# A recurrent layer on one core: the order in which four interleaved streams issue their operations

## The chip, the core and the metric

The kernel runs on one core of a Trainium2 chip. A core has several engines that run side by side, each through its own queue of instructions, in order: TensorE (PE in the profile; its weight loads are PEld), VectorE (DVE), ScalarE (ACT) and GpSimd (POOL); SyncE (SP) issues most of the transfers. An instruction that needs another engine's result waits at the head of its queue for a semaphore, and all that is behind it in that queue waits too. The metric is the time of one execution on the device in microseconds (us); lower is better.

## The reference

The input x has 256 x 256 positions and 32 channels. Four layers are added to it one after another, each on a group-normalised copy: a gated layer, two Sobel layers, and a recurrent one. The last sets most of the time, and the change is in it. It runs over 256 steps (one for each column of x), on 256 sequences (one for each row), with hidden width 128 and two stacked cells:

```python
z = x_t @ W_lat + b_lat
for j in range(2):
    zz = concatenate([z, h_all[j]], axis=1) @ W_cell[j] + b_cell[j]
    zz = group_norm(zz)                      # 4 groups of 128, one for each gate
    i, f, o, g = split(zz, 4, axis=1)
    c = sigmoid(f) * c_all[j] + sigmoid(i) * tanh(g)
    h = sigmoid(o) * tanh(c)
    z = z + h
x_hat = x_t + z @ W_out + b_out
```

Step t needs h and c of step t-1, so the steps of one cell can't overlap; the two cells and the two halves of the sequences can.

## The kernel before

The recurrence (`recurrence`) works on **four streams**: layer l in (0, 1) times half h in (0, 1) of the sequences, 128 sequences each, on 128 partitions. One step of one stream is a chain of short operations. They have short names, and this document writes the stream behind the name: `sq01` is the square of layer 0, half 1.

- **PE**: `m` multiplies the stream's last hidden state by its recurrent weights (L911), `i` multiplies the hidden state of layer 0 by layer 1's weights (L906, only in streams 10 and 11). Both add into `zz`, one PSUM bank of 128 x 512. `T` transposes by the identity (L963), `to` does so with the output gate (L959, only in the "turned" streams 00 and 10). Once per step `project` (called `x` here, L876 and L879) puts the input's part into the `zz` of all four streams; its matmuls have 32 rows and run four abreast.
- **ACT**: `sq` squares `zz` (L919); `si`, `sf`, `so`, `tg` are the four gates, scaled by the normalisation (L900); `th` is tanh of c (L966).
- **DVE**: `rd` sums the squares of each gate (L924), `ig` = sigmoid(i) tanh(g) (L947), `fc` = sigmoid(f) c (L951), `c` adds the two (L955), `h` = sigmoid(o) tanh(c) (L969 in turned streams, L973 in the others), `e` copies the transposed h out of PSUM (L975, streams 01 and 11). Once per step `hs` adds the h of both layers (L986).
- **POOL**: `pw` raises the sums to the power -1/2 (L927).

In a turned stream c and the output gate are transposed first (`to`, `T`), then tanh and the product are taken; in the others h is computed first and then transposed (`T`, `e`).

Every 8 steps an **output block** is made (`emit`): `o0` multiplies two blocks of the layer's input (L998, one full matmul), `o1` adds the hidden states' part (L1008, matmuls of 32 columns that run four abreast), `of` moves the sum from PSUM to `fin` on ACT (L1017), `ot` transposes it on DVE (L1023), and DMAs on SP's queue store it.

**The order is written by hand.** `PLAN` gives every operation of every stream a moment in us, `PERIOD` the distance of two steps, `OUT` the moments of `x`, `hs` and the output's four parts. All operations of all steps are sorted by these moments and issued in that order; each engine gets its own subsequence. A moment has no other meaning: no operation waits for it. What an operation waits for are semaphores, and what stands ahead of it in its own engine's queue. Moments over PERIOD only mean that the streams are at different steps: at any time stream 11 is two to three steps behind stream 00.

Buffers: the eight PSUM banks are handed out from a list, first in, first out (`bank`, `release`); a `zz` bank comes free with the last of its four gates, a transpose's bank with `h` or `e`, the output's with `of`. Gates, products and tanh have four buffers each (`up`, bufs=4), one for each stream; `sums` and `roots` have 32 slots per stream (`SLOTS`), so from step 32 on `rd` also has to know that `pw` of 32 steps ago has read its slot.

The functions around the change, with the line numbers of the profile:

Of the kernel before, what the change touches and what calls it, by code (L numbers as in the profile page):

```python
# [19 lines left out]
T = 256  # L20
# [723 lines left out]
class RecurrentInputs:  # L744
# [33 lines left out]
    def of(self, t, rows):  # L778
# [5 lines left out]


SLOTS = 32
PERIOD = 7.600
BLOCKS = 2
PLAN = {
    (0, 0): dict(  # L790
        m=0.300, sq=1.814, rd=1.883, pw=2.686, tg=4.187, sf=4.207, so=4.930, fc=5.023,
        to=5.301, si=5.390, ig=5.646, c=5.897, T=6.647, th=7.011, h=7.161,
    ),
    (0, 1): dict(
        m=4.328, sq=5.425, rd=6.234, pw=8.247, sf=8.370, tg=8.501, si=8.549, fc=8.711,
        so=8.739, ig=9.246, c=9.459, th=9.581, h=10.106, T=10.657, e=11.627,
    ),
    (1, 0): dict(
        i=10.749, m=14.225, sq=14.912, rd=15.578, pw=16.964, si=17.174, so=17.198, tg=17.865,
        to=17.992, ig=18.493, sf=18.507, fc=18.957, c=19.359, T=19.440, th=19.713, h=20.542,  # L800
    ),
    (1, 1): dict(
        i=17.550, m=17.552, sq=18.681, rd=19.727, pw=20.540, si=20.935, sf=21.284, fc=21.803,
        tg=21.870, ig=21.907, c=22.633, so=23.115, th=23.210, h=23.269, T=23.489, e=24.537,
    ),
}
OUT = dict(x=7.804, hs=31.517, o0=35.554, o1=38.043, of=39.159, ot=39.669)

def recurrence(tc, out, ident, weights, inputs, general):
# [47 lines left out]
    def at(when, what, *args):  # L859
        todo.append((when, len(todo), what, args))  # L860

    first = {k: min(ops[n] for n in ("i", "m") if n in ops) for k, ops in PLAN.items()}
    ahead = {k: floor((when - OUT["x"]) / PERIOD) for k, when in first.items()}
    streams = sorted(first, key=lambda k: first[k] - ahead[k] * PERIOD)

# [168 lines left out]
    for k in range(inputs.NX, NB // inputs.XT):  # L1034
        at(((k - inputs.NX + 1) * inputs.XT * J + 4.0) * PERIOD, inputs.load, k)
    at(-1e5, busy, 6)
    for n in range(min(ahead.values()), T + max(ahead.values())):
        at(n * PERIOD + OUT["x"], project, n)
    for t in range(T):
        for (l, h), ops in PLAN.items():  # L1040
            for name, when in ops.items():
                at(t * PERIOD + when, one, name, l, h, t)
        at(t * PERIOD + OUT["hs"], both, t)
    for blk in range(0, NB, BLOCKS):
        for part in ("o0", "o1", "of", "ot"):
            at(((blk + BLOCKS) * J - 1) * PERIOD + OUT[part], emit, blk, part)
    todo.sort(key=lambda e: e[:2])
# [45 lines left out]
```

## Time and profile before

| | |
|---|---|
| time, median of 3 runs | 2632.47 us (2629.62 to 2633.8) |
| profiled execution, its own time | 2632.46 us |
| its span, first to last instruction | 2630.6 us |
| granted TensorE clock, mean | 0.991 |
| first `sq00` of the recurrence | 630.6 us after the span's start |
| busy share of the span | PE 98%, DVE 89%, ACT 87%, POOL 49% |
| an ordinary step, from step 32 on (median distance of two `T01`) | 7.51 us |
| an ordinary step before step 32 | 7.37 us |
| a step with an output block, from step 32 on | 9.14 us |
| output blocks | 32, of which the last is made when the streams have ended |

The recurrence thus takes some 2000 us of the 2631. A step has 13 operations of PE (one `x` counted as one), 24 of ACT, 23 of DVE and 4 of POOL, and the same pattern repeats: what holds for one ordinary step and for one output block holds for nearly all. In the timeline that is quoted below, columns are start and duration in us, engine, line, operation, output and inputs, shapes and count, and in brackets the engine's idle time ahead with what ended it.

### The profile page before, as it was taken

Reading aid. Unit: us, or ns where it says so; the run is one execution under the profiler, and the core shown is the slowest. Engines: PE = TensorE matmul, PEld = TensorE weight load, DVE = VectorE, ACT = ScalarE, POOL = GpSimd, SP = SyncE. Lnnn points to the kernel's source line nnn. Section 1 sums busy time; section 2 is a strip of 40 time slices with the busy share of each in tenths; the row PEclk is TensorE's granted clock in tenths of the full one; section 3 lists DMA queues with packets and bytes.
Section 4 is the critical chain, followed back from the end, with each engine's and each line's share of the span. In section 5 each row is a group of like instructions: output and inputs, shape, how many; then the busy total and the mean of one; then the engine's idle time right before and its main releaser. Section 6 shows DMA issues by size and latency. Waiting matters only on the chain.

```text
span 2630.6 us, 43062 instructions
## 1 busy us (share of the span) xinstructions
PE 2574.9 (98%) x11181; PEld 1007.4 (38%) x11181; DVE 2329.4 (89%) x6735; ACT 2296.4 (87%) x6948; POOL 1298.0 (49%) x1288
## 2 busy tenths in 40 slices
PE   7999999998999999999999999999999999999997
PEld 4533433433333333333333333333333333333332
DVE  6788799796999999999999999999999999999996
ACT  5677677675999999999999999999999999999996
POOL 2211276463555555555555555555555555555553
PEclk9899999999999999999999999999999999999998
DMA  4000000002010000001010101010000001000000
GB/s 146 1 1 1 18 1 1 0 1 49 1 25 8 18 12 14 16 10 20 6 21 5 21 5 21 5 24 9 18 12 14 16 10 20 6 5 5 5 5 10
DMA packets 110744, 38.68 MB, mean 15 GB/s; under 512 B 74852, under 2 KB 107653, under 8 KB 110488
## 3 DMA queue, kind: packets, MB, share of 16 engines
q1 hardware_dynamic: 108452, 34.54, 6.1%
q8 instruction: 92, 1.51, 0.3%
q14 instruction: 164, 1.34, 0.2%
q10 hardware_dynamic: 1236, 0.99, 0.1%
q0 software_dynamic: 800, 0.30, 0.1%
HBM read 10.63 MB, written 8.39 MB: 7 GB/s over the span
## 4 chain that ended last, share of the span: by engine, by line
PE 93%; DVE 3%; ACT 2%; POOL 1%; issue 1%; DMA 1%; DVEq 0%; SPq 0%; ACTq 0%; POOLq 0%
PE zz L911 35%; PE zz L906 16%; PE zz L879 8%; PE pt L963 6%; PE pv L315 5%; PE pg L489 4%; PE pg L449 3%; PE zz L876 3%; PE pg L339 2%; PE pt L959 2%; PE pg L315 1%; PE px L1008 1%; PE pc L259 1%; PE px L998 1%; PE pb L280 1%
## 5 line engine op out<-in xcount | busy, mean ns | idle before, releaser
L927 POOL TENSOR_TENSOR rs<-ve,mhalf 128x4 f32<-128x4 f32 x1024 | 1047.1, 1023 | 953.5 <-DVE ve L924 953.5
L911 PE MATMUL zz<-wc,hT 128*128 128x512 f32 x2040 | 1069.0, 612 | 1.4 <-DVE hT L969 1.2
L900 ACT ACTIVATE ga<-zz,rs 128x128 f32<-128x128 f32 x3072 | 974.7, 376 | 53.6 <-POOL rs L927 47.3
L924 DVE TENSOR_REDUCE ve<-sq 128x4 f32<-128x516 f32 x1024 | 705.2, 689 | 69.4 <-ACT sq L919 49.1
L919 ACT ACTIVATE sq<-zz 128x512 f32<-128x512 f32 x1024 | 623.7, 609 | 53.8 <-PE zz L911 14.2
L906 PE MATMUL zz<-wc,hT 128*128 128x512 f32 x1024 | 524.4, 594 | 0.0
L911 PEld LDWEIGHTS zz<-wc,hT 128*128 128x128 f32 x2040 | 306.7, 189 | 355.8 <-DVE hT L969 168.7
L900 ACT ACTIVATE go<-zz,rs 128x128 f32<-128x128 f32 x1024 | 394.1, 385 | 0.0
L947 DVE TENSOR_TENSOR c<-ga 128x128 f32<-128x128 f32 x1024 | 298.4, 291 | 65.1 <-ACT ga L900 58.6
L951 DVE TENSOR_TENSOR fc<-ga,c 128x128 f32<-128x128 f32 x1020 | 297.9, 292 | 5.5 <-ACT ga L900 4.1
L955 DVE TENSOR_TENSOR c<-c,fc 128x128 f32<-128x128 f32 x1020 | 286.7, 281 | 8.8
L879 PE MATMUL zz<-fx,xt 32*128 32x512 f32 x2048 | 265.8, 589 | 0.0
L333 DVE TENSOR_TENSOR o<-pv,sg 128x512 f32<-128x512 f32 x256 | 158.1, 681 | 43.3 <-PE pg L315 37.7
L959 PEld LDWEIGHTS pt<-ident,go 128*128 128x128 f32 x512 | 71.1, 139 | 290.8 <-ACT go L900 283.4
L906 PEld LDWEIGHTS zz<-wc,hT 128*128 128x128 f32 x1024 | 172.7, 209 | 9.4 <-issue 9.4
L963 PEld LDWEIGHTS pt<-ident,c 128*128 128x128 f32 x512 | 70.9, 139 | 268.9 <-DVE c L955 260.9
L966 ACT ACTIVATE th<-c 128x128 f32<-128x128 f32 x512 | 166.0, 324 | 4.6 <-DVE c L955 1.2
L963 PE MATMUL pt<-ident,h 128*128 128x128 f32 x512 | 157.9, 308 | 10.8 <-DVE h L973 8.5
L330 ACT ACTIVATE sg<-pg 128x512 f32<-128x512 f32 x256 | 138.6, 599 | 31.0 <-PE pg L315 26.3
L966 ACT ACTIVATE th<-pt 128x128 f32<-128x128 f32 x512 | 146.2, 286 | 18.9 <-PE pt L963 18.9
L969 DVE TENSOR_TENSOR hT<-pt,th 128x128 f32<-128x128 f32 x512 | 144.1, 282 | 13.8 <-ACT th L966 13.8
L315 PE MATMUL pv<-xb,wv 32*128 32x512 f32 x512 | 156.2, 619 | 0.0
(169 smaller groups left out, 2991.6 us busy)
## 6 DMA issues: line engine op xcount, KB each, us to landing
xt<-xa SPq DMA_DIRECT2D x256, 64.0 KB, 2.0
nat<-in_x_dram SPq DMA_DIRECT2D x16, 512.0 KB, 7.1
out_dram<-st SPq DMA_DIRECT2D x252, 32.0 KB, 1.7
wc<-in_L_conv_W_cell_dram SPq DMA_DIRECT2D x2, 512.0 KB, 4.8
kt<-in_consts_dram ACTq DMA_DIRECT2D x1, 832.0 KB, 6.1
wv<-in_L_conv_Wv_dram POOLq DMA_DIRECT2D x4, 32.0 KB, 4.2
wg<-in_L_conv_Wg_dram POOLq DMA_DIRECT2D x4, 32.0 KB, 6.2
out_dram<-st ACTq DMA_DIRECT2D x4, 32.0 KB, 3.3
```

What stands on the lines that cost most here:

```text
L315: nc.tensor.matmul(ps, lhsT=w[rows, half * P : (half + 1) * P], rhs=mn, start=True, stop=True)
L879: nc.tensor.matmul(v["zz", l, h, t], lhsT=inputs.of(t, r), rhs=fx[r, :], start=False, stop=l == 0 and t == 0,)
L900: nc.scalar.activation(dst, gates(x, g), func, scale=scale)
L906: nc.tensor.matmul(get("zz"), lhsT=v["hT", 0, t][:, seqs], rhs=wc[:, l, 0, :], start=False, stop=t == 0)
L911: nc.tensor.matmul(get("zz"), lhsT=v["hT", l, t - 1][:, seqs], rhs=wc[:, l, 1, :], start=False, stop=True,)
L919: nc.scalar.activation(sqs[l, h][:, :, 0:H], four(get("zz")), AF.Square, scale=float(H**-0.5))
L924: nc.vector.tensor_reduce(ve, sqs[l, h], AX.X, ALU.add)
L927: nc.gpsimd.tensor_tensor(rs, get("ve"), inputs.mhalf, ALU.pow)
L947: nc.vector.tensor_mul(c, gates(get("ga"), 0), gates(get("ga"), 2))
L951: nc.vector.tensor_mul(fc, gates(get("ga"), 1), get("c"))
L963: nc.tensor.transpose(get("pt")[:, 1, 0:P], get("c" if turned else "h"), ident)
L966: nc.scalar.activation(th, get("pt")[:, 1, 0:P] if turned else get("c"), AF.Tanh)
```

## The change

The change gives other moments to the operations. No operation is added, removed or altered.

```diff
-PERIOD = 7.600
+PERIOD = 7.6
 BLOCKS = 2
 PLAN = {
     (0, 0): dict(
-        m=0.300, sq=1.814, rd=1.883, pw=2.686, tg=4.187, sf=4.207, so=4.930, fc=5.023,
-        to=5.301, si=5.390, ig=5.646, c=5.897, T=6.647, th=7.011, h=7.161,
+        m=0.300, sq=0.897, rd=1.315, pw=1.564, sf=2.898, si=3.787, fc=4.372, so=4.652,
+        tg=4.729, ig=5.014, c=5.113, to=5.590, T=6.355, th=6.448, h=6.513,
     ),
     (0, 1): dict(
-        m=4.328, sq=5.425, rd=6.234, pw=8.247, sf=8.370, tg=8.501, si=8.549, fc=8.711,
-        so=8.739, ig=9.246, c=9.459, th=9.581, h=10.106, T=10.657, e=11.627,
+        m=4.745, sq=4.953, rd=5.207, pw=5.217, tg=7.548, sf=7.918, si=8.072, so=8.125,
+        fc=8.561, ig=8.685, c=8.879, th=9.050, h=10.132, T=10.974, e=11.085,
     ),
     (1, 0): dict(
-        i=10.749, m=14.225, sq=14.912, rd=15.578, pw=16.964, si=17.174, so=17.198, tg=17.865,
-        to=17.992, ig=18.493, sf=18.507, fc=18.957, c=19.359, T=19.440, th=19.713, h=20.542,
+        i=11.096, m=13.564, sq=14.380, rd=14.501, pw=14.603, so=16.610, tg=16.973, to=17.142,
+        sf=17.184, si=17.445, fc=18.142, ig=18.269, c=18.830, T=19.003, th=19.210, h=19.658,
     ),
     (1, 1): dict(
-        i=17.550, m=17.552, sq=18.681, rd=19.727, pw=20.540, si=20.935, sf=21.284, fc=21.803,
-        tg=21.870, ig=21.907, c=22.633, so=23.115, th=23.210, h=23.269, T=23.489, e=24.537,
+        i=16.893, m=17.050, sq=17.642, rd=19.345, pw=20.086, si=21.131, sf=21.350, tg=21.355,
+        fc=21.369, ig=21.584, c=21.731, so=22.208, th=22.427, h=23.006, T=23.391, e=23.986,
     ),
 }
-OUT = dict(x=7.804, hs=31.517, o0=35.554, o1=38.043, of=39.159, ot=39.669)
+OUT = dict(x=7.281, hs=31.329, o0=30.902, o1=34.402, of=35.065, ot=35.363)
```

Only the order counts, so the moments are to be sorted. Taken modulo PERIOD they give each engine's order within one step. Each row begins where the lists are easiest to compare and runs round; the output's parts, which come in one step of eight, are in brackets.

```
PE   before  m00      T11 i11 m11 to10 T01 i10 T10      m01 [o0] to00 m10 T00 [o1] x
PE   after   m00 [o0] T11 i11 m11 to10 T01 i10 T10 [o1] m01      to00 m10 T00      x
ACT  before  [of] sq00 si10 th01 so10 tg10 sf10 sq11 tg00 sf00 th10 so00      si00 sq01 si11 sf11 tg11 th00 sq10 so11 th11 sf01 tg01 si01 so01
ACT  after        sq00 so10 th01 tg10 sf10 si10 sq11 sf00 si00 th10 so00 [of] tg00 sq01 si11 sf11 tg11 th00 sq10 so11 th11 tg01 sf01 si01 so01
DVE  before  rd00 h01 ig10 fc10 e01 c10 rd11 fc00 h10      ig00 c00 rd01 fc11 ig11 h00 c11 rd10 h11 fc01 hs ig01 [ot] e11 c01
DVE  after   rd00 h01 fc10 ig10 e01 c10 rd11 fc00 h10 [ot] ig00 c00 rd01 fc11 ig11 h00 c11 rd10 h11 hs fc01 ig01      e11 c01
POOL both    pw00 pw11 pw01 pw10
```

Before, `of` and `ot` of a block are issued in the step after its `o0` and `o1`; after, all four parts are in one step; their moments are 3.6 to 4.7 us earlier.

## The prediction

> **What bounds the kernel now.** I read the page first (busy time, the chain that ended last), then the timeline of one ordinary step, then that of a step with an output block.
>
> ```profile
> PE 2574.9 (98%) x11181; PEld 1007.4 (38%) x11181; DVE 2329.4 (89%) x6735; ACT 2296.4 (87%) x6948; POOL 1298.0 (49%) x1288
> PE 93%; DVE 3%; ACT 2%; POOL 1%; issue 1%; DMA 1%; DVEq 0%; SPq 0%; ACTq 0%; POOLq 0%
> ```
>
> This says PE, but matmuls overlap in the trace, so a busy PE need not be a full one. The timeline of an ordinary step shows what sets its length:
>
> ```profile
> 1238.42 0.30 PE L963 MATMUL pt<-ident,h 128*128 128x128 f32 x1
> ...
> 1239.53 1.02 PE L911 MATMUL zz<-wc,hT 128*128 128x512 f32 x2
> ...
> 1240.65 0.60 ACT L919 ACTIVATE sq<-zz 128x512 f32<-128x512 f32 x1
> ...
> 1241.35 0.69 DVE L924 TENSOR_REDUCE ve<-sq 128x4 f32<-128x516 f32 x1 [0.17 <-ACT sq L919]
> ...
> 1242.58 0.27 DVE L955 TENSOR_TENSOR c<-c,fc 128x128 f32<-128x128 f32 x1
> ...
> 1242.76 1.13 PE L911 MATMUL zz<-wc,hT 128*128 128x512 f32 x2
> ...
> 1242.95 0.31 ACT L966 ACTIVATE th<-c 128x128 f32<-128x128 f32 x1
> 1243.17 0.88 ACT L900 ACTIVATE ga<-zz,rs 128x128 f32<-128x128 f32 x3
> ...
> 1243.73 0.33 PE L963 MATMUL pt<-ident,h 128*128 128x128 f32 x1
> ...
> 1243.93 0.38 ACT L900 ACTIVATE go<-zz,rs 128x128 f32<-128x128 f32 x1
> 1244.18 0.61 ACT L919 ACTIVATE sq<-zz 128x512 f32<-128x512 f32 x1
> ...
> 1244.89 0.69 DVE L924 TENSOR_REDUCE ve<-sq 128x4 f32<-128x516 f32 x1
> ...
> 1245.50 0.28 DVE L973 TENSOR_TENSOR h<-go,th 128x128 f32<-128x128 f32 x1
> ...
> 1245.93 0.30 PE L963 MATMUL pt<-ident,h 128*128 128x128 f32 x1
> ```
>
> Read as a ring: T01 starts at 1238.42; behind it in PE's queue come i10 (+0.14), T10 (+0.86) and m01 (+0.11, 1239.53). m01 ends at 1240.55; sq01 waits for it (1240.65), rd01 for sq01 (1241.35). Behind rd01 stand fc11, ig11, h00 and c11 in DVE's queue (1242.58, ends 1242.85). th11 waits for c11 (1242.95); the gates of 01 and sq00 stand behind it on ACT (1244.18, ends 1244.79). rd00 waits for sq00 (1244.89), h01 stands behind rd00, and T01 waits for h01: 1245.93. **The ring closes after 7.51 us, the step's length**, and has no slack. PE waits in it: the same step's distances without waits (six full matmuls at 0.86, six transposes at 0.11, x with its entry and exit 0.10 + 1.18 + 0.10) sum to 5.16 + 0.66 + 1.38 = 7.20, so PE loses 0.31 per step, most of it ahead of T01.
>
> In a step with an output block another path binds:
>
> ```profile
> 1208.73 1.02 PE L998 MATMUL px<-xa,e 128*128 128x512 f32 x2
> ...
> 1210.56 0.27 PE L963 MATMUL pt<-ident,c 128*128 128x128 f32 x1
> ...
> 1210.76 1.07 PE L1008 MATMUL px<-hs,wout 128*32 128x256 f32 x16
> ...
> 1211.76 0.40 PE L876 MATMUL zz<-fb,sel 32*128 32x512 bf16 x4
> ...
> 1213.04 0.72 ACT L1017 ACTIVATE fin<-px,cst 128x512 f32<-128x512 f32 x1
> ...
> 1213.79 0.71 DVE L1023 STREAM_TRANSPOSE st<-fin 128x512 f32<-128x512 f32 x1 [0.35 <-ACT fin L1017]
> ...
> 1214.17 0.60 ACT L919 ACTIVATE sq<-zz 128x512 f32<-128x512 f32 x1 [0.41 <-PE zz L911]
> ...
> 1215.90 0.30 PE L963 MATMUL pt<-ident,h 128*128 128x128 f32 x1
> ```
>
> o0 takes 0.86 of PE and o1 1.00 (1210.76 to 1211.76), back to back with the rest. T01 comes at 1206.76 and again at 1215.90: 9.14 us, 1.63 over an ordinary step though 1.86 of PE was added; part fell into PE's waits. of and ot cost nothing: of runs while ACT would wait for PE's m00 anyway (sq00 still waits 0.41 after it).
>
> **What the Trainium skill says.** "Perfetto Trace Analysis", Identifying the Most-Contended Engine: matmul busy time is no measure of how full TensorE is. The trace agrees: 98% busy, 0.31 of 7.51 lost. The same page, Identifying Dependency Chains: an instruction that waits for several engines may get extra EventSemaphore instructions ahead of it. Visible here: up to step 31 rd starts 0.03 after its sq (709.56 + 0.60, then 710.19), from step 32 on 0.10, and each rd then has an EVENT_SEMAPHORE ahead of it; the step goes from 7.37 to 7.51 (two rd in the ring, 0.07 each). "TensorEngine Tiling (Array Packing)", Key Properties: a change of tiling mode drains TensorE. Here T00 to o1 takes 0.20 (1210.56 to 1210.76) against 0.11 between untiled instructions, and m00 after x holds PE for 0.97 instead of 0.86. "SBUF — State Buffer", Who interferes with whom: a VectorE instruction with two SBUF inputs and a GpSimd instruction that reads SBUF block one another. At most pw11 shows it, 1.09 at 1239.93 against 1.01 for the other three; 0.08, and not in the ring.
>
> **The change, part by part.**
>
> *Ordinary steps.* Take each link of the ring into the new order. PE: T01, i10, T10, m01 unchanged. DVE: rd01, fc11, ig11, h00, c11 unchanged; rd00, h01 unchanged. ACT: between th11 and sq00 stand the same four gates, tg01 ahead of sf01 instead of behind it. All other links are data. So the ring has the same instructions, and **the ordinary step can't become shorter than 7.51** unless a wait itself becomes cheaper. Could another path become longer?
> - so10 goes from third to first behind sq00, 0.45 earlier. to10 waits less, but T01 behind it still waits for h01: gain 0.
> - so10 is then the first to need pw10, which ends at 1237.06, 0.09 before si10 starts now: covered, and if it weren't, ACT would lose under 0.1 ahead of sq11.
> - si10 goes behind sf10, and fc10 and ig10 swap with it: c10 has the same four gates ahead of it. tg00 goes last of stream 00 and takes si00's place ahead of ig00: same again. Both hidden; without this cover 0.25 each (one gate).
> - hs ahead of fc01: 0.34 sooner on DVE, fc01 later by as much; e11, c01 and rd00 have the same work ahead. If ig01 came late, rd00 (0.07 of idle before it) would slip.
> - An extra event wait may come to th01, since the gate that opens stream 10 is now another one: 0.07, against 0.03 of room behind, and 0.25 until h01 needs it. I take 0.
>
> Sum for ordinary steps: 0, bounds -0.02 and +0.02.
>
> *o0* is moved from behind m01 to behind m00. It now delays T11, i11, m11, to10 and T01. T01 to m00 is 4.34 (1238.42 to 1242.76); then m00 0.97, o0 0.86, T11 0.11, i11 0.86, m11 0.86, to10 0.11: T01 to T01 is 8.11, that is **+0.60**. VectorE is ready by then: T11's turn is 1.83 after m00, e11 is done 0.63 later (as e01 after T01, 1238.42 to 1239.05), then c01 0.20, rd00 0.60, h01 0.20: 3.46, and T01's turn is 3.77.
>
> *o1* is moved from between T00 and x to between T10 and m01, **into the ring**. T01 to m01 becomes i10's 0.11 + 0.86 + 0.20 (T10, with the change of mode) + 1.00 (o1) = 2.17 against 1.11: **+1.06**. Leaving o1's mode may cost m01 another 0.10, as x does to m00; see below.
>
> *of and ot* now follow o1 at once, ahead of tg00 on ACT and of ig00, c00 and **rd01** on DVE. From the turn of m01: o1's recorded end +0.07, of starts 0.12 later (the last block, where ACT was idle: 2621.38 to 2621.50), takes 0.72, ot starts 0.03 later and takes 0.71: 1.65. Behind it ig00 (+0.20), c00 (+0.33, it waits for ig00), rd01 (+0.60): rd01 ends 2.78 after m01's turn. Ordinarily it ends 2.51 after (1239.53 to 1242.04). **+0.27**; the possible 0.10 on m01 lies under it (2.61). Bounds: with ot hidden only that 0.10 stays; with ACT or DVE later than I count, 0.40.
>
> Queues: of's wait for o1 holds up tg00 and sq01 on ACT; tg00 is through 0.91 + 0.26 = 1.17 after m01's turn, and sq01 waits for m01 until 1.12 to 1.22 anyhow. On SP only the output's eight DMAs move with ot; x's loads have steps of room. POOL keeps its order.
>
> *Sum.* After, a block costs 0.60 + 1.06 + 0.27 = 1.93; before, 1.63: **+0.30**. 31 blocks run inside the recurrence: 9.3 us. In the first three the step is 0.14 and sq01 to rd01 0.07 shorter, so they cost 2.14 after against 1.71 before (9.08 less 7.37), 0.13 more each: 0.4. The last block stands alone at the end in both orders. Together +9.7, on the profiled 2632.46 (2630.6 and 1.9 around it), which equals the median 2632.47: **2642 us**, 0.37% slower.
>
> **The rivals.**
> - *Of and ot hidden after all* (13%): the block costs 1.66 to 1.76, +0.03 to +0.13, 1 to 4 us: 2633.5 to 2637, no change. For it: DVE stands still ahead of ot anyway. Against: rd01 is behind ot in the queue.
> - *A double wait leaves the ring* (9%), the faster side: th11 starts 0.10 after c11's end where th01 starts 0.03 after c01's (1214.88 to 1214.91), an event wait's price; if the new order spares it (or one of sq01, rd, T01), 0.07 x 225 steps = 16 us, more than the 9.7: 2626. It decides from 0.06 per step. Against: each of these has the same predecessors in the new order.
> - *A double wait enters the ring* (8%): +16, 2658, the same arithmetic.
> - *The order has no effect* would need o1 outside the ring; its new place is read off the list.
>
> **How the numbers follow.** The forecast has 70% (2638 to 2647). Range 2635 to 2649: the forecast, the nearer half of the hidden case and some of the extra waits. A run can't tell less than about 0.2% (5.3 us) from no change. Faster 0.09, same 0.14, slower 0.77.
>
> **What would show it.** Ordinary T01 to T01 still 7.51 (else the ring argument falls); the block's excess 1.9 over the two steps that it touches; rd01 right behind c00 with ot ahead of ig00; o1 between T10 and m01. An ordinary step off by 0.03 would make the forecast wrong.

## The result, and the profile after

The kernel after takes 2642.98 us (median of 7 runs, 2636.38 to 2648.2), beside 2631.05 us for the kernel before (also 7 runs). The medians are 11.9 us apart; the ratio, taken over all runs, is 1.0036 (95% interval 1.0026 to 1.0046), 9.5 us slower. Its profiled execution took 2636.38 us, with a span of 2634.5 us. Measured again later beside more runs of the kernel before, the ratio was 1.0022 (1.0014 to 1.0030), 5.8 us.

Runs of one kernel differ with the TensorE clock that each was granted. Of the 20 runs of the kernel before in the second measurement, the seven at 0.991 have a median of 2631.3 us, the six at 0.989 one of 2636.3. **At equal clock the kernel after is about 7 us slower**: 7.5 at 0.991 (2638.8, seven runs), 6.9 at 0.989 (2643.2, four runs). In the first measurement four of its seven runs had 0.989, with a median of 2643.0, so at that clock it took the same time in both. The 2631.05 beside it is what the kernel before takes at 0.991; the clocks of those runs, the profiled one (0.991) apart, are not on record. So the 9.5 seems to be in part a difference of granted clocks.

The page of the kernel after says as little as that of before: first the engines' busy times, then the chain that ended last.

```profile
PE 2579.5 (98%) x11181; PEld 1012.0 (38%) x11181; DVE 2318.2 (88%) x6735; ACT 2304.8 (87%) x6948; POOL 1282.6 (49%) x1288
...
PE 93%; DVE 3%; ACT 2%; POOL 1%; issue 1%; DMA 1%; DVEq 0%; SPq 0%; ACTq 0%; POOLq 0%
```

The timeline of one ordinary step of the kernel after (start, duration, engine, line, operation) shows the ring again, link by link:

```profile
1238.01 0.30 PE L963 MATMUL pt<-ident,h 128*128 128x128 f32 x1
...
1239.12 1.02 PE L911 MATMUL zz<-wc,hT 128*128 128x512 f32 x2
...
1240.24 0.60 ACT L919 ACTIVATE sq<-zz 128x512 f32<-128x512 f32 x1
...
1240.94 0.69 DVE L924 TENSOR_REDUCE ve<-sq 128x4 f32<-128x516 f32 x1 [0.18 <-ACT sq L919]
...
1242.17 0.27 DVE L955 TENSOR_TENSOR c<-c,fc 128x128 f32<-128x128 f32 x1
...
1242.54 0.31 ACT L966 ACTIVATE th<-c 128x128 f32<-128x128 f32 x1
1242.75 0.88 ACT L900 ACTIVATE ga<-zz,rs 128x128 f32<-128x128 f32 x3
...
1243.76 0.61 ACT L919 ACTIVATE sq<-zz 128x512 f32<-128x512 f32 x1
...
1244.48 0.69 DVE L924 TENSOR_REDUCE ve<-sq 128x4 f32<-128x516 f32 x1
...
1245.08 0.28 DVE L973 TENSOR_TENSOR h<-go,th 128x128 f32<-128x128 f32 x1
...
1245.51 0.30 PE L963 MATMUL pt<-ident,h 128*128 128x128 f32 x1
```

From `T01` (1238.01) to `T01` (1245.51) is 7.50 us, and 7.51 before. `m01` comes 1.11 behind `T01`, `sq01` 1.12 behind `m01`, `rd01` 0.70 behind `sq01`: the same distances as before, so the new order left the ring alone.

The two steps with an output block, again from the timeline of the kernel after:

```profile
1508.83 0.30 PE L963 MATMUL pt<-ident,h 128*128 128x128 f32 x1
...
1514.12 1.02 PE L998 MATMUL px<-xa,e 128*128 128x512 f32 x2
...
1516.91 0.27 PE L963 MATMUL pt<-ident,h 128*128 128x128 f32 x1
...
1517.88 0.27 PE L963 MATMUL pt<-ident,c 128*128 128x128 f32 x1
...
1518.09 1.07 PE L1008 MATMUL px<-hs,wout 128*32 128x256 f32 x16
...
1519.09 1.13 PE L911 MATMUL zz<-wc,hT 128*128 128x512 f32 x2
1519.22 0.69 ACT L1017 ACTIVATE fin<-px,cst 128x512 f32<-128x512 f32 x1 [0.50 <-PE px L1008]
...
1519.94 0.71 DVE L1023 STREAM_TRANSPOSE st<-fin 128x512 f32<-128x512 f32 x1 [1.09 <-ACT fin L1017]
...
1520.31 0.60 ACT L919 ACTIVATE sq<-zz 128x512 f32<-128x512 f32 x1
1520.58 0.25 DVE L947 TENSOR_TENSOR c<-ga 128x128 f32<-128x128 f32 x1
...
1520.86 0.29 DVE L955 TENSOR_TENSOR c<-c,fc 128x128 f32<-128x128 f32 x1
1521.07 0.68 DVE L924 TENSOR_REDUCE ve<-sq 128x4 f32<-128x516 f32 x1
...
1525.64 0.30 PE L963 MATMUL pt<-ident,h 128*128 128x128 f32 x1
```

The step with `o0` takes 8.08 (1508.83 to 1516.91), the step with `o1`, `of` and `ot` 8.73 (to 1525.64). Together they are 1.80 over two ordinary steps, where a block cost 1.64 before: 0.17 more (1.803 less 1.637), 31 times, is 5.2 us. From the first `T01` of the recurrence to the last it is 1971.2 us after and 1964.2 before, in the profiled executions: 7.0 us.

### The profile page after: what moved, and what is told of

The parts are those of the page before. It is cut to its first block, busy times and chain, and to the rows that moved or that the text cites. A ratio compares the mean times of both kernels' runs of the same rounds, so it can differ in the third digit from the quotient of the medians.

```text
span 2634.5 us, 43253 instructions
## 1 busy us (share of the span) xinstructions
PE 2579.5 (98%) x11181; PEld 1012.0 (38%) x11181; DVE 2318.2 (88%) x6735; ACT 2304.8 (87%) x6948; POOL 1282.6 (49%) x1288
## 4 chain that ended last, share of the span: by engine, by line
PE 93%; DVE 3%; ACT 2%; POOL 1%; issue 1%; DMA 1%; DVEq 0%; SPq 0%; ACTq 0%; POOLq 0%
PE zz L911 35%; PE zz L906 17%; PE zz L879 8%; PE pt L963 6%; PE pv L315 5%; PE pg L489 4%; PE pg L449 3%; PE zz L876 3%; PE pg L339 2%; PE pt L959 2%; PE px L1008 1%; PE pg L315 1%; PE pc L259 1%; PE px L998 1%; PE pb L280 1%
## 5 line engine op out<-in xcount | busy, mean ns | idle before, releaser
L927 POOL TENSOR_TENSOR rs<-ve,mhalf 128x4 f32<-128x4 f32 x1024 | 1031.3, 1007 | 977.3 <-DVE ve L924 977.3
L900 ACT ACTIVATE ga<-zz,rs 128x128 f32<-128x128 f32 x3072 | 931.0, 369 | 47.8 <-POOL rs L927 40.4
L951 DVE TENSOR_TENSOR fc<-ga,c 128x128 f32<-128x128 f32 x1020 | 289.1, 283 | 16.2 <-ACT ga L900 9.7
L963 PEld LDWEIGHTS pt<-ident,h 128*128 128x128 f32 x512 | 71.1, 139 | 289.1 <-DVE h L973 159.1
L975 DVE COPY hT<-pt 128x128 f32<-128x128 f32 x512 | 145.9, 285 | 15.0 <-PE pt L963 14.8
```

The lines of the kernel that those rows point to most:

```text
L900: nc.scalar.activation(dst, gates(x, g), func, scale=scale)
L927: nc.gpsimd.tensor_tensor(rs, get("ve"), inputs.mhalf, ALU.pow)
L951: nc.vector.tensor_mul(fc, gates(get("ga"), 1), get("c"))
L963: nc.tensor.transpose(get("pt")[:, 1, 0:P], get("c" if turned else "h"), ident)
```

## The experiments

The ratio in the table is against the kernel before, measured on the same chip in the same stretch; its medians there were 2631.1 to 2634.9 us.

| run | time, us | ratio (95% interval) | ordinary step | a block's excess |
|---|---|---|---|---|
| before | 2632.5 | 1 | 7.51 | 1.64 |
| after | 2643.0 | 1.0036 (1.0026 to 1.0046) | 7.50 | 1.80 |
| after, again | 2639.0 | 1.0022 (1.0014 to 1.0030) | 7.50 | 1.81 |
| outputs alone moved | 2638.4 | 1.0010 (1.0002 to 1.0018) | 7.50 | 1.81 |
| gates alone moved | 2633.9 | 0.9997 (0.9990 to 1.0003) | 7.50 | 1.64 |
| after, `of` and `ot` late | 2671.3 | 1.0133 (1.0118 to 1.0149) | 7.50 | 2.84 |
| after, `ot` alone late | 2655.9 | 1.0082 (1.0069 to 1.0096) | 7.50 | 2.37 |
| after, 128 places for sums | 2647.3 | 1.0045 (1.0031 to 1.0059) | 7.54 | 1.88 |
| after, 8 tanh buffers | 2636.3 | 1.0010 (1.0001 to 1.0018) | 7.50 | 1.81 |
| before, 4 places in layer 1 | 2604.4 | 0.9892 (0.9877 to 0.9907) | 7.36 | 1.71 |
| before, five double waits out | 2587.5 | 0.9826 (0.9813 to 0.9840) | 7.30 | 1.77 |
| the same, `hs` moved | 2589.9 | 0.9830 (0.9815 to 0.9845) | 7.32 | 1.76 |
| the same, outputs moved | 2603.1 | 0.9876 (0.9860 to 0.9892) | 7.30 | 2.14 |

The last two columns are medians from each run's trace: the distance of two `T01` from step 32 on, and by how much the steps that a block touches, with the one behind them, are longer than that in all.

### Which part of the change costs: the outputs or the gates

Theory: the outputs' four parts make the whole difference, the other moves change nothing. Rival: the gates' order costs, or wins, a wait in every step. First the outputs' places alone, in the kernel before:

```diff
-OUT = dict(x=7.804, hs=31.517, o0=35.554, o1=38.043, of=39.159, ot=39.669)
+OUT = dict(x=7.804, hs=31.517, o0=30.900, o1=34.700, of=35.600, ot=36.000)
```

> The kernel before with the four parts of the output block alone at their new places (o0 behind m00, o1 between T10 and m01, of ahead of the last gate of stream 00, ot between h10 and ig00); the gates and products keep their old order. Ring theory: ordinary steps 7.51 us, a block costs what it costs in the changed kernel, 0.58 in the step with o0 and 1.23 in the next, 1.81 in all against 1.64 before; 31 x 0.17 = 5 to 6 us over the kernel before, +0.2%. Rival, that the new order of the gates costs the time: block excess 1.64, equal to the kernel before within 1 us.

Then everything else alone: the kernel after, with the outputs at places equal to those of before.

```diff
-OUT = dict(x=7.281, hs=31.329, o0=30.902, o1=34.402, of=35.065, ot=35.363)
+OUT = dict(x=7.281, hs=31.329, o0=35.700, o1=37.400, of=38.600, ot=39.150)
```

> The changed kernel with the output's four parts back at their old places among the other operations (o0 behind m01, o1 behind T00, of ahead of sq00, ot ahead of e11 of the next step). Ring theory: ordinary steps 7.51, block excess 1.64, as in the kernel before: 0 to +3 us, the 3 for stalls of 0.15 us that the changed kernel's ScalarE shows at tg01 every 15 steps and the kernel before seldom shows at that place. Rival, that the gates' order costs the time: the whole +9 us stay.

The outputs alone gave 1.0010 (+2.6 us, 0.5 to 4.7) and in the trace the pattern of after: steps of 8.09 and 8.73, excess 1.81. The ratio is below what was expected, but these runs had a higher clock (mostly 0.991 and 0.992) than the runs of before beside them (mostly 0.988 and 0.989). At 0.991 they took 2638.7 (six runs) against 2632.4 (four): +6.3 us, as in the traces (1970.4 from the first `T01` to the last, against 1964.2). The gates alone gave 0.9997 and the pattern of before, excess 1.64; at 0.991 they took 2633.7 (eleven runs), +1.3 us. So the new order of the gates, of `hs` and of `fc` against `ig` changes neither the ordinary step nor the block, and the outputs' places carry nearly the whole difference. What the 1.3 us can be stands in the part on the stalls below.

### What `of` and `ot` cost where they stand now

In the kernel after, `of` and `ot` were put back to their old places, first both, then `ot` alone.

```diff
-OUT = dict(x=7.281, hs=31.329, o0=30.902, o1=34.402, of=35.065, ot=35.363)
+OUT = dict(x=7.281, hs=31.329, o0=30.902, o1=34.402, of=38.600, ot=39.150)
```

> The changed kernel with of and ot alone back at their old places in the next step (of between so01 and sq00, ot between ig01 and e11); o0 and o1 stay where the change put them. If the old place was free whatever else is moved: the block loses the 0.16 that ot now costs, or the part of it that m01's slow start doesn't cost anyway, 0.06 to 0.16, some 2 to 5 us less than the changed kernel. Ring theory: the old place was covered only by PE's late m00, which came from o1 behind T00; with o1 in the ring that cover is gone, of and ot stand in the ring one behind the other, and a step gets 0.9 to 1.05 longer: 28 to 32 us more than the changed kernel, about 2670.

```diff
-OUT = dict(x=7.281, hs=31.329, o0=30.902, o1=34.402, of=35.065, ot=35.363)
+OUT = dict(x=7.281, hs=31.329, o0=30.902, o1=34.402, of=35.065, ot=39.150)
```

> The kernel after with ot alone back at its old place, 4 us later; of stays where it is. What the step of the prediction on of and ot then says: rd01 no longer stands behind ot, so its 0.27 per block falls to the 0.10 of the slower start of m01 behind o1: -0.17 x 31 = -5 us against after. From the trace of after: rd01 ends 0.157 late, 0.10 of which is m01's: the block's excess falls from 1.80 to 1.75, -1.8 us, about 0.07% below after, hard to see in the times but plain in the profile (8.73 becomes 8.67). If of holds sq01 up by itself: no change.

With both late the time came out as expected, 2671 us (but not for the reason expected, see below). With `ot` alone late it did not: 2656 us instead of a little less than after. Both traces settle the disputed size all the same. `rd01` ends 2.511 us after `m01`'s turn in an ordinary step and 2.668 in the block's step of after. With `ot` late it ends 2.613 after it, with both late 2.612. So of the 0.157, **0.10 is `m01`'s slow start** behind `o1`'s other tiling mode (in the lines above, `m01` is 1.13 long at 1519.09 and 1.02 in an ordinary step), and **0.055 is `ot`**. The expectation had that part right (0.05 was named), but missed what the old place costs. The timeline of the run with `ot` alone late, in the step after the block:

```profile
1535.65 0.28 DVE L947 TENSOR_TENSOR c<-ga 128x128 f32<-128x128 f32 x1
...
1535.95 0.71 DVE L1023 STREAM_TRANSPOSE st<-fin 128x512 f32<-128x512 f32 x1
...
1536.59 0.25 DVE L975 COPY hT<-pt 128x128 f32<-128x128 f32 x1
...
1536.89 1.13 PE L911 MATMUL zz<-wc,hT 128*128 128x512 f32 x2 [0.48 <-DVE hT L975]
```

`ot` stands ahead of `e11` and `c01` here; PE waits 0.48 for `e11`'s copy, and `rd00` and `h01` come 0.57 later. In the kernel before, the same place is free, because VectorE waits there for `sq00`, which waits for a late `m00`: `o1` stood just ahead of `x` and `m00`. The place was covered by `o1`'s old place, and the change moves `o1` away. The step is 9.22 instead of 8.73.

With `of` late too, one more thing shows, which the expectation had not named. The timeline of that run:

```profile
1540.87 0.39 PE L876 MATMUL zz<-fb,sel 32*128 32x512 bf16 x3
...
1542.02 0.37 PE L876 MATMUL zz<-fb,sel 32*128 32x512 bf16 x1 [0.76 <-DVE hT L969]
...
1542.02 1.23 PE L879 MATMUL zz<-fx,xt 32*128 32x512 f32 x8
...
1543.48 0.70 ACT L1017 ACTIVATE fin<-px,cst 128x512 f32<-128x512 f32 x1
...
1544.40 0.60 ACT L919 ACTIVATE sq<-zz 128x512 f32<-128x512 f32 x1 [0.22 <-PE zz L911]
```

Only three of `x`'s four streams start; the fourth waits 1.14 us, until `h00` has ended and given back a transpose's bank. In the kernel after, the list of banks gives `x` the output's bank, which `of` has released by then. So `of` behind `o1` also hands back a PSUM bank in time, and `m00` would be late without it. `of` has ended at 1544.18, and `sq00` starts 0.22 later, when the late `m00` is done: the wait that ends last is the one for the bank, and not the one for `of` in ScalarE's queue that was expected. That the size was as expected is in part luck.

### The doubled waits in the ring

A double wait is the wait of one instruction for two engines, with an event wait (an EVENT_SEMAPHORE instruction) ahead of it for one of them. The prediction's rival on the faster side was that one of these leaves the ring. It didn't, but the price could be tested by taking such waits out. First, in the kernel after, 128 places instead of 32 for the sums of the two streams of layer 0, so that `rd00` and `rd01` don't wait for a `pw` up to step 127:

```diff
-    sums = kp.tile([P, 2 * L, SLOTS, 4], F32, name="ve")
+    sums = {
+        (l, h): kp.tile([P, SLOTS if l else 4 * SLOTS, 4], F32, name=f"ve{l}{h}")
...
-            ve = v["ve", l, h] = sums[:, 2 * l + h, t % SLOTS, :]
+            ve = v["ve", l, h] = sums[l, h][:, t % (SLOTS if l else 4 * SLOTS), :]
```

> The changed kernel with 128 instead of 32 slots of sums for the two streams of layer 0, so that rd00 and rd01 need no second wait before step 128. Ring theory: the ordinary step stays at 7.37 until step 127 instead of step 31 and is 7.51 from 128 on: 96 steps x 0.135 = 13 us less than the changed kernel, and the block's cost is unchanged. Rival, that the step from 7.37 to 7.51 comes from something else that grows with time: the change stays near step 32, equal time.

A miss: 2647 us, slower than after, and 7.54 per step from step 32 on. The timeline of an ordinary step (line numbers are 4 higher from the edit on, so `pw` is L931 and `rd` L928):

```profile
1245.62 0.60 ACT L923 ACTIVATE sq<-zz 128x512 f32<-128x512 f32 x1
...
1246.24 0.69 DVE L928 TENSOR_REDUCE ve<-sq 128x4 f32<-128x516 f32 x1
...
1247.08 1.12 POOL L931 TENSOR_TENSOR rs<-ve,mhalf 128x4 f32<-128x4 f32 x1 [1.12 <-DVE ve L928]
...
1247.83 0.31 ACT L970 ACTIVATE th<-c 128x128 f32<-128x128 f32 x1
1248.23 0.88 ACT L904 ACTIVATE ga<-zz,rs 128x128 f32<-128x128 f32 x3
```

`rd01` does start 0.03 behind `sq01` (1246.24) instead of 0.10. But now `pw01` has the event wait: it starts 0.14 behind `rd01`'s end instead of 0.08, and lasts 1.12 instead of 1.01. It ends at 1248.20, and the first gate of stream 01 starts at 1248.23, 0.09 after `th11` has ended; ordinarily the gate starts 0.09 before `th11`'s end. **A second path runs beside the ring**: `rd01`, `pw01`, the first gate of stream 01. In the kernels before and after the gate starts 0.042 behind `pw01`'s end, and an instruction that only waits for `pw01` starts 0.034 behind it: the room is 0.01. The wait that left `rd01` came back on `pw01` (the trace of this run has an event wait ahead of `pw01` and of `pw00` in each step, that of after none), since `rd`'s wait for an old `pw` had also covered the reuse of the places of `roots`.

Two runs looked at this path from both sides. One takes only `th11`'s double wait out, in the kernel after:

```diff
-            th = v["th", l, h] = up.tile([P, H], F32, name="th")
+            th = v["th", l, h] = up.tile([P, H], F32, name="th", bufs=8)
```

> The kernel after, with eight buffers for the tanh tile instead of four. In the compiled program th11, th01 and th00 then wait for one engine only, so ScalarE issues 31 instead of 34 instructions per step. Theory A (only the ring of fc11, c11, th11 sets the step): th11 starts 0.03 instead of 0.10 behind c11, the ordinary step falls by 0.07 from 7.51 to 7.44, 225 steps, -16 us: about 2627. Theory B (a second path runs beside it, rd01 to pw01 to the first gate of stream 01, with 0.017 of room): the step falls by 0.02 only, to 7.49, -4 us: about 2639. On the stalls of about 0.15 us that come on the first gate of stream 01 every 15 steps (512 ScalarE instructions at 34 per step): if they are tied to the count of instructions, they now come every 16.5 steps and wander over the operations, and fewer fall on the ring.

`th11` then starts 0.034 behind `c11` instead of 0.094, but the ordinary step stays at 7.50: the gate behind it now starts 0.034 behind `pw01`. Theory B holds, with even less than was expected of it. (The time is lower than that of after: at 0.991 it is 3.8 us over the kernel before, 2635.4 in eight runs against 2631.6 in six. More on this under the stalls.)

The other gives the sums and roots of *layer 1* fewer places, in the kernel before:

```diff
-    sums = kp.tile([P, 2 * L, SLOTS, 4], F32, name="ve")
-    roots = kp.tile([P, 2 * L, SLOTS, 4], F32, name="rs")
+    sums, roots = (
+        {
+            (l, h): kp.tile([P, 4 if l else SLOTS, 4], F32, name=f"{n}{l}{h}")
+            for l in range(L)
+            for h in range(2)
+        }
+        for n in ("ve", "rs")
+    )
...
-            ve = v["ve", l, h] = sums[:, 2 * l + h, t % SLOTS, :]
+            ve = v["ve", l, h] = sums[l, h][:, t % (4 if l else SLOTS), :]
...
-            rs = v["rs", l, h] = roots[:, 2 * l + h, t % SLOTS, :]
+            rs = v["rs", l, h] = roots[l, h][:, t % (4 if l else SLOTS), :]
```

`rd11` and `rd10`, which are not in the ring, then wait for a recent `pw`, four steps old. VectorE's queue is in order, so it knows from that wait that the older `pw` of layer 0 has ended too, and neither `rd01` nor `rd00` nor `pw01` needs a second wait of its own.

> The kernel before, with 4 instead of 32 places for the sums and roots of the two streams of layer 1; those of layer 0 keep 32. In the compiled program rd11 and rd10 wait for a pw of four steps earlier from the fifth step on, and rd01 and rd00 then wait for ScalarE alone: their event wait is gone in every step. pw01 and pw00 keep one wait each. Theory: the two waits of 0.07 are what made 7.37 into 7.51 from step 32 on; the ordinary step stays 7.37 to the end, block excess 1.70 as in the first 32 steps: 224 x 0.135 = 30 us less, 2 us given back in 27 blocks: 0.9894 of before, some 2606. Rival (the run with 128 places: another wait takes the place of the one removed): the step returns to 7.5 and nothing is gained, 2632 to 2637.

2604.4 us, 0.9892 of before, as expected (2606). The ordinary step is 7.36 to the end. Its timeline (line numbers 6 higher):

```profile
1235.51 0.60 ACT L925 ACTIVATE sq<-zz 128x512 f32<-128x512 f32 x1
...
1236.14 0.69 DVE L930 TENSOR_REDUCE ve<-sq 128x4 f32<-128x516 f32 x1
...
1236.91 1.01 POOL L933 TENSOR_TENSOR rs<-ve,mhalf 128x4 f32<-128x4 f32 x1 [1.03 <-DVE ve L930]
...
1237.74 0.31 ACT L972 ACTIVATE th<-c 128x128 f32<-128x128 f32 x1
1237.96 0.87 ACT L906 ACTIVATE ga<-zz,rs 128x128 f32<-128x128 f32 x3
```

`rd01` starts 0.03 behind `sq01`, `pw01` 0.08 behind `rd01` and lasts 1.01: nothing has come back. Two event waits of 0.07 in the ring are what makes 7.37 into 7.51 from step 32 on.

The next run adds two squares tiles in turn for each stream of layer 0 (so `sq00` and `sq01` no longer wait for ScalarE's own older square), and two tanh tiles in turn for stream 11 (`sq` writes with the same index as `rd` reads):

```diff
-                sq = self.sqs[l, h] = kp.tile([P, 4, H + 1], F32, name=f"sq{l}{h}")
+                sq = self.sqs[l, h] = kp.tile([P, 1 if l else 2, 4, H + 1], F32, name=f"sq{l}{h}")
...
-            nc.vector.tensor_reduce(ve, sqs[l, h], AX.X, ALU.add)
+            nc.vector.tensor_reduce(ve, sqs[l, h][:, 0 if l else t % 2], AX.X, ALU.add)
...
-            th = v["th", l, h] = up.tile([P, H], F32, name="th")
+            th = v["th", l, h] = up.tile([P, H], F32, name=f"th{l}{h}", bufs=1 + l * h)
```

> The kernel before with three things: 4 places for the sums and roots of layer 1 as in the run beside it; two squares tiles in turn for each of the streams of layer 0; two tanh tiles in turn for stream 11, one for each other stream. In the compiled program sq00, sq01, rd00, rd01 and th11 then wait for one engine each: all five doubled waits of the ring are gone. Theory: 0.135 from rd00 and rd01, 0.14 from sq00 and sq01, at most 0.07 from th11 (0.02 by the second path over pw01): 7.51 to between 7.16 and 7.22, but TensorE's own work per step is 7.20, so 7.20 to 7.25; a block then costs what TensorE spends on it, 1.9 to 2.1 instead of 1.64. -0.28 x 224 - 0.15 x 32 + 0.4 x 31 = -55 us, about 2578 (2570 to 2592). Rival: VectorE or ScalarE hold the step at 7.35 to 7.4 some other way, 2600 to 2610.

2587.5 us: inside the range named, 10 us above its likeliest value. The step is 7.30, not 7.20 to 7.25. `sq01` gave what was expected: it starts 0.038 behind `m01`'s end instead of 0.098. `sq00` gave nothing: it stands behind the four gates in ScalarE's queue and doesn't wait for its data, and from `rd01`'s end to `sq00` it is 2.13 with and without its event wait. `th11` gave nothing either, since the gate behind it starts 0.034 behind `pw01`. VectorE, too, has no gap now from `rd10` to `h01`. So the next run moves `hs` out of that stretch, to where VectorE stands still:

```diff
-OUT = dict(x=7.804, hs=31.517, o0=35.554, o1=38.043, of=39.159, ot=39.669)
+OUT = dict(x=7.804, hs=35.900, o0=35.554, o1=38.043, of=39.159, ot=39.669)
```

> The run with all five doubled waits out of the ring (7.30 per step, 2587.5 us), with the sum hs moved from between fc01 and ig01 to between h10 and ig00, where VectorE stands still for 0.22 us. In the run without the move VectorE has no gap from rd01 to h01, so the ring now runs through its queue and hs (0.20 to its successor) stands in it. Theory: the step falls to TensorE's own 7.20 to 7.22 (-0.08 to -0.10 x 256 = -20 to -26 us), a block rises by as much (+0.08 x 31 = +2.5): 2564 to 2570. Rival (the room ahead of ig00 is used up by waits that follow): 7.26 to 7.30, 2577 to 2587.

A miss again, outside both ranges, and the rival was nearer: 7.32 and 2589.9 us. VectorE does get its gap back, but the path over `pw01` alone holds the step. The timeline (line numbers 6 higher):

```profile
1242.60 1.01 POOL L933 TENSOR_TENSOR rs<-ve,mhalf 128x4 f32<-128x4 f32 x1 [0.98 <-DVE ve L930]
...
1243.38 0.31 ACT L972 ACTIVATE th<-c 128x128 f32<-128x128 f32 x1
...
1243.64 0.89 ACT L906 ACTIVATE ga<-zz,rs 128x128 f32<-128x128 f32 x3
```

`pw01` ends at 1243.61 and the gate starts at 1243.64. ScalarE was free for it 0.05 earlier: where a gate only has to wait for `th11`, it starts 0.09 before the recorded end of `th11`, here 0.05 before it. The run with five double waits out is the fastest of the study, 45 us below the kernel before.

Last, the change's places for the outputs in that freed kernel, one step later since `hs` is later:

```diff
-OUT = dict(x=7.804, hs=35.900, o0=35.554, o1=38.043, of=39.159, ot=39.669)
+OUT = dict(x=7.804, hs=35.900, o0=38.500, o1=42.300, of=43.200, ot=43.600)
```

> The run beside it (doubled waits out of the ring, hs moved), with the change's places for the outputs, one step later as hs now comes later: o0 behind m00, o1 between T10 and m01, of behind so00, ot ahead of ig00. Where TensorE sets the ordinary step, a block costs at least its TensorE time: 0.86 + 1.00 + 0.20 = 2.06. In the old places some of this falls into the wait ahead of T01 that a block leaves (about 1.87). Theory: in the new places 0.86 + 1.07 + 0.16 = 2.09, +0.2 x 31 = +6 us against the run beside it, so the change of the outputs costs about the same here as in the kernel before. Rival (the cost came from the ring, which has no longer the last word): within 2 us of the run beside it.

It costs more there than in the kernel before: 13 us in the medians (10 at equal clock: 2589.1 and 2599.4 at 0.991, three runs and two), 8.5 us in the traces (first `T01` to last: 1925.2 and 1933.7). The rival, within 2 us, falls. A block costs 2.14 (8.09 and 8.66 against two of 7.30) instead of 1.76. The step of the old order with a block takes 9.09 in all three freed kernels, where the ordinary step is 7.36, 7.30 or 7.32, and 9.14 in the kernel before: the old places let PE run through, so the block's step is set by PE alone. In the new places PE has a wait that the expectation had not named. The timeline (line numbers 6 higher):

```profile
1639.19 0.71 DVE L1029 STREAM_TRANSPOSE st<-fin 128x512 f32<-128x512 f32 x1 [0.76 <-ACT fin L1023]
...
1639.40 1.02 PE L917 MATMUL zz<-wc,hT 128*128 128x512 f32 x2
...
1640.11 0.29 DVE L961 TENSOR_TENSOR c<-c,fc 128x128 f32<-128x128 f32 x1
...
1640.46 0.33 PE L969 MATMUL pt<-ident,c 128*128 128x128 f32 x1
```

`T00` waits for `c00`, which stands behind `ot` and `ig00` in VectorE's queue. It starts 1.06 behind `m10` (1639.40) instead of 0.86, and `x` follows it after 0.26 instead of 0.20. This wait of about 0.25 and the two changes of tiling mode (0.09 ahead of `o1`, 0.10 at `m01`) come to 0.44, a little more than the 0.38 by which a block costs more here than in the old places. The length of the ring has little to do with it: a block's two steps take 16.75, and 16.81 in after, although the ordinary step has become 0.20 shorter. In after `T00` comes as late (1.05 behind `m10`), but there `T01` waits for `h01` until 0.08 to 0.09 after TensorE is ready for it, so the wait ahead of `T00` stays hidden.

### The rest: a stall of ScalarE that keeps step with the order

Some steps without an output's part, from step 32 on, are 0.06 to 0.5 too long: 21 in the trace of after (4.0 us in all), 12 in that of before (2.9 us). With the gates alone moved it is 25 (4.6 us), with the outputs alone moved 12 (2.9 us): the new order of the gates brings the additional ones, and their 1 to 2 us are of the size of the 1.3 us above. Many of those of after are alike. Here is the same place as in the ordinary step above, in step 72 of after (timeline):

```profile
1188.05 0.31 ACT L966 ACTIVATE th<-c 128x128 f32<-128x128 f32 x1
1188.42 0.89 ACT L900 ACTIVATE ga<-zz,rs 128x128 f32<-128x128 f32 x3
```

From `th11` to `tg01` it is 0.37 instead of 0.21 (1242.54 to 1242.75). The same 0.15 comes at `tg01` in steps 42, 57, 72 and so on to 252, every 15 steps. In the kernel after, ScalarE's trace has 34 instructions per step, event waits counted (33 before; `th01` has a double wait now), and 15 steps with their two `of` make 512. In the kernel before, 8 steps with their `of` make 265, and the 512th lands on another operation each time. Most of these are on time, `tg01` of steps 74 and 244 too, which has no event wait there. Only three are late, by 0.27 to 0.28: `sq01` of step 28, `th11` of 103 and `sq11` of 119, each with an event wait ahead of it, as `tg01` has one in after. With eight tanh buffers (above) ScalarE issues 31 per step; all stalls at `tg01` are gone, as expected, and 9 long steps remain, 2.0 us in all. So the stall goes with the count of instructions, but not every instruction at that count is late. That it takes an event wait fits these cases and was not tested; what causes it is not shown. The page of after lists two DMA queues that carry instructions:

```profile
q8 instruction: 92, 1.51, 0.2%
q14 instruction: 166, 1.36, 0.2%
```

(Columns: packets, MB, share of 16 engines.) In the trace of after, a packet of 8 KB on q14 starts 0.6 to 0.9 us behind 14 of the 15 late `tg01`; of the other 208 `tg01` from step 30 to 252 the same is true of 14. So the stalls keep step with the supply of instructions. The packet starts after the late gate, so it is not shown that the gate waits for it, and no run tested this.

Because the first measurement of after was above what the trace holds, the kernel ran once more, unchanged:

> The kernel after, unchanged, once more beside runs of the kernel before on the same chip. The traces account for +5.2 us from the blocks (0.17 x 31) and about +0.6 from more stalls on the ring; the first measurement gave +9.5 (6.9 to 12.1), the run with the outputs alone +2.6 (0.5 to 4.7). If the trace's account is whole: 1.0015 to 1.0030 (+4 to +8 us). If something that the traces don't show adds to it: 1.0036 or more again.

1.0022, +5.8 us, inside the range for the trace's account. Its trace has the same steps (7.50, 8.08, 8.73), and the long ones of after come again, 4.1 us in all. At equal clock it is +6.9 to +7.5 us (see the result), the 7.0 of the traces. The outputs alone (+6.3) and the gates alone (+1.3) add up to this too.

## Why the prediction was right

*Ordinary steps: 0.* Right. 7.50 after, and 7.50 with the gates' order alone; the ring argument held, and the gates alone gave 0.9997 of the time.

*o0: +0.60.* Right: 0.58 (8.08 to 8.09 against 7.50).

*o1, into the ring: +1.06.* Right to the hundredth: `T01` to `m01` is 2.173 in the block's step and 1.107 in an ordinary one.

*Of and ot: +0.27, bounds 0.10 and 0.40.* Right in kind and inside the bounds, but too large: 0.157. This is the term that was mis-sized. `ot` ended 1.57 us after `m01`'s turn, not 1.65 (`of` took 0.69 and not 0.72, and started 0.14 behind that turn, not 0.19), and `ig00` to `rd01` took 1.10 behind it, not 1.13. Since 0.10 would have been lost to `m01`'s slow start anyway, which two runs showed, `ot` itself costs 0.055. The prediction had that 0.10 as lying under the 0.27; it turned out to be most of the cost. The prediction followed `ot` only to `rd01`. Its other follower, `T00` behind `c00`, was not counted; it missed being the longer path by 0.08 to 0.09 us. "TensorEngine Tiling (Array Packing)", Key Properties, in the Trainium skill tells of the drain at a change of mode; this case prices it, 0.10 to enter (`T10` to `o1` is 0.21 in the lines of after, 1517.88 to 1518.09, where untiled instructions follow a transpose by 0.11) and 0.10 to leave.

*The sum: +9.7.* A block costs 1.80 and not 1.93, and cost 1.64 before and not 1.63: +0.17 instead of +0.30, so 5.2 us instead of 9.3. The first three blocks added 0.6 instead of 0.4 (one of them has a stall of 0.27 in it), and the stalls in the other steps 1.1, which the prediction didn't know. That makes 6.9 of the 7.0 that the profiled recurrence grew by. That 2642 met the first median within 1 us is thus luck: the predicted +9.7 was counted from a run at a clock of 0.991, where the kernel after took 2638.8 in the repeat, and four of the seven runs behind the median had 0.989. The better figure is 7 us; the sign and the mechanism are the prediction's.

*The rivals.* "Of and ot hidden" claimed a block of 1.66 to 1.76; it was 1.80, nearer to it than to the 1.93, but not hidden. "A double wait leaves the ring" did not happen. Its arithmetic was half right: 0.07 x 225 holds for `rd01` and `rd00` (two of them gave 28 us), but for `th11`, the example that was given, it would have brought about 1 us, because `pw01` was 0.01 behind it. The prediction's statement that the ring has no slack was true, but it did not ask whether another path has as little.

*The event wait at th01* did come. `th01` starts 0.094 behind `c01` in an ordinary step, and 0.078 in the kernel before; the 0.03 of the prediction was read in a step with a block. `h01` was not later, so the wait cost nothing at its own place, as taken. It changed the count of instructions, and with it where the stalls fall.

## What to carry to other kernels

Put work that comes in one step of several where the engine that issues it already waits, and check what else covers that wait: the old place of `of` and `ot` was free only as long as `o1` stood ahead of `m00`. Before pricing the removal of a wait from a ring, look for the next path through the same instructions and measure its room (0.01 us here); and see whether the wait goes or moves. A second wait can be had for nothing if an instruction outside the ring, ahead in the same queue, already waits for something later from that engine: four places instead of 32 made this kernel 1.1% faster.

## What the runs showed of the hardware that was not expected

- An event wait ahead of an instruction that is held by its data costs 0.06 to 0.07 us: 0.069 at `rd`, 0.060 at `sq01`, 0.060 at `th11`, 0.064 at `pw01`. Ahead of `sq00`, which is held by its queue, it costs nothing.
- ScalarE lost 0.15 us at `tg01` every 512 instructions of its queue in the kernel after, and 0.27 to 0.28 at three of the operations at that count in the kernel before; all of these have an event wait ahead of them, and the others at that count lost nothing (above). VectorE has a like stall of 0.35 to 0.38 us: in the kernels before and after and in the run with eight tanh buffers alike, `rd10` of steps 46 and 83, `rd11` of step 50, `rd00` of steps 57 and 94 and `rd01` of steps 177 and 214 start so late. Each `rd` has an event wait ahead of it, and the distances between these, counted in VectorE's instructions, are multiples of 128 (128, 128, 768, 256, 2304, 1024). Whether the count is the cause is not shown here either.
- A `pw` of the same four columns lasted 1.01 in most runs but 1.12 on stream 01 with 128 places for the sums. On stream 11 it lasted 1.08 in the kernel before and with the outputs alone moved, and 1.01 in the kernel after and with the gates alone moved, so this goes with the order of the gates. Why is not shown.
